# Second attention's row sums taken from the channel sum of its result, with values raised by one and the residual lowered by one

## The chip, the cores and the metric

The kernel runs on one core of a Trainium2 chip. The metric is the device time of one execution in microseconds; the median of three runs stands for a kernel. Profiles come from one further execution.

## The reference, cut to what matters

The input x has 8 batches of 128 channels on 48 x 48 positions, all in fp32. With N = 2304 tokens in a batch, the reference computes:

```python
# layer 0: causal attention with projections of the group-normed input
x0 = concat([gn(x), pe])
q, k, v = lrelu(Wq x0 + bq), lrelu(Wk x0 + bk), lrelu(Wv x0 + bv)
attn = softmax(mask(q.T k / sqrt(128))) * mask
x = x + attn v
# layer 1: attention of the normed tokens with themselves, no weights
t = to_tokens(x)                      # (8, 2304, 128)
h = ln(t)                             # over the 128 channels, no scale, no offset
t = t + softmax(h h.T) h
# FFN: product with W, batch statistics over all tokens, a recurrence over tokens
wx = batch_norm(ln(t) W.T)
y[n] = sigmoid(wx[n] + y[n - 1] V.T)
x = from_tokens(t + y)
```

For the change, two facts of the second attention count. Its score matrix h h.T is symmetric. And the 128 channels of each row of h, being layer-normed without an offset, add up to zero.

## The kernel before, in words

A batch's 2304 tokens are cut into NQ = 6 chunks of QC = 384 tokens, and each chunk into QB = 3 blocks of 128. Both attentions take one chunk of queries after the other. For each block of keys a score matmul gives s (128 keys by 384 queries) in PSUM, ScalarE takes the exponential into p, and a product matmul adds p times the values into o, which holds channels by queries in PSUM. No maximum is taken. The denominators are row sums of p, applied to o after it has been turned so that tokens lie on the partitions.

**Order of the work.** `fast_path` (L605) writes the order of all instructions by hand. The main loop (L1418 to L1446) goes through one list of items, (chunk, block) pairs of all batches; in each step it issues the score of item n (`begin`), the product of item n - 3 (`product`, LAG = 3) and at a chunk's end `after`. Everything else is put in as chains of steps: `Stream` (L548) is a planner with modelled costs of VectorE, ScalarE and GpSimd, and `tick` issues up to two steps whose modelled due time has come after each item. Costs that the code gives a step thus decide where later steps stand. The list of batch b + 1 begins before that of batch b has ended: its first three causal items lie among the last six items of batch b.

**Projections.** `project` (L855) makes q, k and v of a chunk: `normed` (L872), three matmuls pj (L879 and L882), for each an addition z (L884) on VectorE that frees the PSUM bank, and the leaky ReLU (L889). Scores s and projections pj share a pool of four PSUM banks (`ps_s`); turned results share one of two (`ps_t`), and o has two. Tiles p come from a pool of six.

**First attention.** `Causal` (L989): score L1018, exponential L1020, on the diagonal blocks a mask on GpSimd (L1023), product L1029. Its denominators are added up on VectorE in acc (L1040, L1044), and at a chunk's end summed (`turn` L1069 and L1071; `sums` L1077 to L1082, with a matmul against `same`, a matrix that adds up groups of partitions, and a mask `mine` that keeps a partition's own group). `residual` (L1091) gives t1, token by channel, held in t1_tok; moments, a root on GpSimd (L929) and `normed` (L934) give h, stored token major as x_hat[b][0] (xhT in the profile, the values of the second attention), and `back` transposes it into x_hat[b][1] (xh, its queries and keys).

**Second attention.** `Full` (L1123). Since the scores are symmetric, the exponentials of a pair of chunks i < j are made once, as direct tiles (score L1219, exponential L1221 with the running row sums `accum_out` into rows, product L1233). Each such tile is also turned by VectorE in 32 x 32 squares (L1182) into t, stored to DRAM as e (L1162), loaded as g (L1153) and used for the other chunk of the pair (product L1229, "turned"). For every three turned tiles one VectorE reduce (L1190) adds up the sums of the turned part into tsum.

At a chunk's end `after` (L1239) copies o to SBUF (L1251) and adds a chain of steps. `sums` reduces rows (L1259); for chunks 0 to 4 it multiplies tsum by `same` (ts, L1264), keeps its own groups (own, L1269), reduces and adds them (more, L1273, L1274); the reciprocal (L1276) is ri. `residual` turns the result by three transposes on TensorE (of_t, L939), forms t2 = of_t x ri + t1 (L1286, three instructions), takes the moments (L920, L921, L923) and turns t2 (tt, L1293). Then come a root on GpSimd (L1299), DRAM transfers that bring t2 back channel major, `product` (matmul wx L1325, its scaling L1326, statistics L1327) and `stored` (a ScalarE copy L1331). The last two chunks of the last batch take a way without DRAM (L1361 to L1372), and then the recurrence (from L1448) begins.

Tiles of the chain are shared: `chunk_tile(tag, name, holder, steps)` makes the planner run the tile's former chain up to `steps` steps before the tile is taken again, and `st.advance(before, 7)` in `keep` does the same for the chain of the chunk before; these counts include the step `sums`.

Of the kernel before, what the change touches and what calls it, by code (L numbers as in the profile page):

```python
# [14 lines left out]
F32 = mybir.dt.float32  # L15
AF = mybir.ActivationFunctionType
# [588 lines left out]
def fast_path(ctx: ExitStack, tc: tile.TileContext, x, pe, w_ffn, out, x_tok, w_qkv, w_pos, v_t, gamma_beta, flag):  # L605
# [61 lines left out]
    with ExitStack() as actx:  # L667
# [93 lines left out]
        for r in range(1 - R, R):  # L761
            nc.gpsimd.affine_select(
                out=same, in_=same, compare_op=ALU.not_equal, fill=1.0, base=r * SQ, pattern=[[0, R], [-1, SQ]], channel_multiplier=1
            )
        mine = apool.tile([P, NQ - 1, R, QB], F32, tag="mine", name="mine")
        nc.gpsimd.memset(mine, 1.0)
        nc.gpsimd.affine_select(
            out=mine, in_=mine, compare_op=ALU.is_ge, fill=0.0, base=0, pattern=[[0, NQ - 1], [-SQ, R], [0, QB]], channel_multiplier=1
        )
        nc.gpsimd.affine_select(  # L770
            out=mine, in_=mine, compare_op=ALU.is_ge, fill=0.0, base=SQ - 1, pattern=[[0, NQ - 1], [SQ, R], [0, QB]], channel_multiplier=-1
        )
# [216 lines left out]
        class Causal:  # L989
# [57 lines left out]
            def after(self, j, o):  # L1047
# [25 lines left out]
                def sums():  # L1073

                    tp = psum_t(f"dn_{b}_{j}")
                    k = R * QB
                    nc.tensor.matmul(tp[:, :k], same.rearrange("p a c -> p (a c)"), c["parts"], start=True, stop=True)  # L1077
                    own = small.tile([P, R, QB], F32, tag="ownc", name=f"ownc_{b}_{j}")
                    nc.vector.tensor_mul(own.rearrange("p a g -> p (a g)"), tp[:, :k], mine[:, 0].rearrange("p a g -> p (a g)"))
                    ri = small.tile([P, QB], F32, tag="ric", name=f"ric_{b}_{j}")  # L1080
                    nc.vector.tensor_reduce(ri, own.rearrange("p a g -> p g a"), AX.X, ALU.add)
                    nc.vector.reciprocal(ri, ri)  # L1082
                    c["ri"] = ri
# [24 lines left out]
                def back():  # L1108
                    tp = transposed(c["y"], f"tb_{b}_{j}")
                    nc.scalar.copy(x_hat[b][1][:, cols], tp[:, :QC])  # L1110

                c["chain"] = normed_chunks[b, j] = st.add([
                    *through[:1],
# [5 lines left out]
                    (normed, 0.0, [("DVE", 1.1)]),  # L1119
                    (back, 0.35, [("ACT", 0.5)]),  # L1120
                ], max(at, st.free["DVE"]) + 0.2 - st.now)

        class Full:  # L1123
# [6 lines left out]
            def __init__(self, b):  # L1130
                self.b = b
                self.tsum, self.tiles, self.stored, self.loaded = {}, {}, {}, {}
                self.pairs = [(i, j) for j in range(NQ) for i in range(j)]
                self.used, self.to_store = 0, deque()
# [38 lines left out]
            def turned(self, j, m, p, ready):  # L1173

                b = self.b
                n, g = divmod(m, QB)
                if g == 0:
                    if len(self.to_store) > 1:
                        self.store()
                    self.tiles[n] = tpool.tile([P, R, QB, QB, SQ], F32, tag="t", name=f"t_{b}_{j}_{n}")  # L1180
                t = self.tiles[n]
                nc.vector.transpose(  # L1182
                    t[:, :, :, g, :].rearrange("p b j r -> p j b r"), p.rearrange("p (j b r) -> p j b r", j=QB, b=R)
                )
                at = st.then(ready, [("DVE", 0.57)])
                if g == QB - 1:
                    self.to_store.append((j, n, t, at))
                    if j not in self.tsum:
                        self.tsum[j] = small2.tile([P, NQ - 1, R * QB], F32, tag="tsum", name=f"tsum_{b}_{j}")
                    nc.vector.tensor_reduce(  # L1190
                        self.tsum[j][:, n - j - 1, :], t.rearrange("p b j m r -> p (b j) (m r)"), AX.X, ALU.add
                    )
                    st.then(at, [("DVE", 1.35)])
                    del self.tiles[n]

            def begin(self, j, what, first):
                b = self.b
                if first and j == 0:
                    self.rows = small2.tile([P, NB, NQ], F32, tag="rows", name=f"rows_{b}")
                if j == 0:  # L1200
# [19 lines left out]
                p = pp.tile([P, QC], F32, tag="p", name=f"p1_{b}_{j}_{m}")  # L1220
                nc.scalar.activation(p, s[:, :QC], AF.Exp, bias=shift, accum_out=self.rows[:, m, j : j + 1])  # L1221
                return p, st.then(st.spend(QC * US), [("ACT", 0.58)])

            def product(self, j, what, o, p, ready, first, last):
# [7 lines left out]
                else:  # L1232
                    nc.tensor.matmul(o[:, :QC], xhT[:, what[1], :], p, start=first, stop=last)  # L1233
                    st.then(ready, [("ACT", 0.2)])
                    if what[1] // QB > j:
# [3 lines left out]
            def after(self, j, o):  # L1239
                b, rows, tsum = self.b, self.rows, self.tsum  # L1240
                cols = ts(j, QC)
# [3 lines left out]
                if far:  # L1245
                    ot = turn_result(o, f"f_{b}_{j}", c, True)
                    at = st.then(st.now, [("DVE", 0.57)])
                    through = token_major(c, ot, f"f_{b}_{j}", "tof", 4)
                else:
                    o_sb = chunk_tile("o", f"of_{b}_{j}", c, 2)  # L1250
                    nc.scalar.copy(o_sb, o[:, :QC])  # L1251
                    at = st.then(st.now, [("ACT", 0.5)])
                    through = []
                F = len(through)

                def sums():

                    dn = small2.tile([P, QB], F32, tag="dn", name=f"dn_{b}_{j}")
                    nc.vector.tensor_reduce(dn, rows[:, QB * j : QB * (j + 1), : j + 1], AX.X, ALU.add)  # L1259
                    n = NQ - 1 - j  # L1260
                    if n:
                        tp = psum_t(f"ts_{b}_{j}")
                        k = n * R * QB
                        nc.tensor.matmul(  # L1264
                            tp[:, :k], same.rearrange("p a c -> p (a c)"), tsum[j][:, :n, :].rearrange("p n k -> p (n k)"),
                            start=True, stop=True,
                        )
                        own = small2.tile([P, NQ - 1, R, QB], F32, tag="own", name=f"own_{b}_{j}")
                        nc.vector.tensor_mul(  # L1269
                            own[:, :n].rearrange("p n a g -> p (n a g)"), tp[:, :k], mine[:, :n].rearrange("p n a g -> p (n a g)")  # L1270
                        )
                        more = small2.tile([P, QB], F32, tag="more", name=f"more_{b}_{j}")
                        nc.vector.tensor_reduce(more, own[:, :n].rearrange("p n a g -> p g (n a)"), AX.X, ALU.add)  # L1273
                        nc.vector.tensor_add(dn, dn, more)  # L1274
                    ri = small.tile([P, QB], F32, tag="ri", name=f"ri_{b}_{j}")
                    nc.vector.reciprocal(ri, dn)  # L1276
                    c["ri"] = ri

                def residual():
                    tp = None if far else transposed(o_sb, f"of_t_{b}_{j}")  # L1280
                    t2 = chunk_tile("t2", f"t2_{b}_{j}", c, 5 if last else 2 + F, bufs=1)
                    for g in range(QB):
# [8 lines left out]
                    if not last:  # L1291
                        c["tt"] = chunk_tile("turn", f"tt_{b}_{j}", c, 5 + F, bufs=1)
                        nc.vector.transpose(  # L1293
# [21 lines left out]
                def fetch():  # L1315
                    c["t2x"] = chunk_tile("t2x", f"t2x_{b}_{j}", c, 7 + F, bufs=1)
                    nc.sync.dma_start(c["t2x"], t2_d[:, b, cols])
                    c["scale"] = chunk_tile("scale", f"scale_{b}_{j}", c, 8 + F, bufs=1)
                    nc.sync.dma_start(c["scale"], c["rs_d"][0].partition_broadcast(P))
# [13 lines left out]
                def normed():  # L1333
                    c["x2"] = chunk_tile("t2x", f"x2_{b}_{j}", c, 6, bufs=1)
                    normalize(c["x2"], c["t2"], c["mv"], c["rs"])
# [3 lines left out]
                def keep(t2x):  # L1339

                    k = j % (SG // SJ)
                    if before is not None:
                        st.advance(before, 7 if k else len(before.steps) + before.done)
                    if k == 0:
# [13 lines left out]
                def back():  # L1358
                    tp = turned_back(c["x2"], f"tx_{b}_{j}")
                    c["xc"] = chunk_tile("scale", f"xc_{b}_{j}", c, 7, bufs=1)  # L1360
                    nc.scalar.copy(c["xc"], tp[:, :QC])  # L1361
# [20 lines left out]
                else:  # L1382
# [8 lines left out]
                    *through,  # L1391
                    (sums, 0.15, [("DVE", 0.8)]),
                    (residual, 0.0 if far else 0.35, [("DVE", 3.2)]),
                    (rooted, 0.0, [("POOL", 0.9)]),
# [242 lines left out]
```

## Time and profile before

| | before |
|---|---|
| median of three runs | 1771.99 us (1771.10 to 1772.96) |
| the profiled execution | 1769.93 us |
| its span, from first to last instruction | 1768.1 us |
| granted TensorE clock, mean | 0.993 |
| TensorE busy | 1739.9 us, 98% of the span |
| VectorE busy | 1299.7 us, 74% |
| ScalarE busy | 762.5 us, 43% |
| GpSimd busy | 194.9 us, 11% |

The page of the profile calls the engines PE (TensorE), PEld (its weight loads, which overlap it), DVE (VectorE), ACT (ScalarE), POOL (GpSimd) and SP (SyncE, which issues DMAs). A row of a group names line, engine, operation, output and inputs by the program's names, partitions x elements and how often; behind the bar stand the busy time, the mean of one in ns, and the engine's idle time just before these instructions with what ended it. A row of the timeline begins with the start in us from the span's start and the length of a run of like instructions. An fp32 matmul shows as two records. Between two starts of a matmul of 384 columns lie some 0.645 us where PE is not interrupted. From one batch to the next the same instruction comes 207.66 us later.

### The profile page before, as it was taken

How to read it: one execution, taken by the hardware profiler on the slowest of the kernel's cores; microseconds unless marked ns; L12 is line 12 of the kernel's file. 1: busy time of each engine (PE TensorE's matmuls, PEld its weight loads, DVE VectorE, ACT ScalarE, POOL GpSimd, SP SyncE). 2: the span in 40 equal slices, each digit the busy share in tenths (PEclk: the TensorE clock that was granted, in tenths of full speed). 3: DMA queues.
4: the chain of work that ended last, by engine and by line, in shares of the span. 5: the costliest groups of instructions: out<-in, count | busy, mean ns of one | idle time of the engine just before them, and what ended most of it. 6: DMA issues, size and time to landing. Idle time of an engine off the chain costs nothing.

```text
span 1768.1 us, 22177 instructions
## 1 busy us (share of the span) xinstructions
PE 1739.9 (98%) x6215; PEld 1092.2 (62%) x6215; DVE 1299.7 (74%) x3355; ACT 762.5 (43%) x1836; POOL 194.9 (11%) x301
## 2 busy tenths in 40 slices
PE   9999999999999999999999999999999999999996
PEld 5666566665666566665666656665666656666565
DVE  4868668876887668786687767876687866877467
ACT  2344434443345434444344443454344543444445
POOL 1110011100110001100111001200011001110006
PEclk8999999999999999999999999999999999999998
DMA  3405672257533584156731575334832468116768
GB/s 141 139 23 182 184 203 93 89 184 193 146 103 121 157 235 130 47 167 183 209 99 68 190 197 157 107 108 157 228 120 77 148 183 217 56 46 199 194 231 217
DMA packets 206056, 262.00 MB, mean 148 GB/s; under 512 B 90113, under 2 KB 175010, under 8 KB 205412
## 3 DMA queue, kind: packets, MB, share of 16 engines
q1 hardware_dynamic: 204972, 257.47, 48.2%
q0 software_dynamic: 720, 2.62, 1.0%
q8 instruction: 52, 0.85, 0.2%
q14 instruction: 80, 0.66, 0.1%
q10 hardware_dynamic: 232, 0.40, 0.1%
HBM read 150.24 MB, written 110.17 MB: 147 GB/s over the span
## 4 chain that ended last, share of the span: by engine, by line
PE 96%; DMA 1%; DVE 1%; ACT 1%; issue 0%; SPq 0%; POOL 0%; ACTq 0%; DVEq 0%; POOLq 0%
PE o L1233 19%; PE s L1219 19%; PE s L1018 17%; PE o L1029 17%; PE o L1229 13%; PE pj L879 4%; PE pj L882 2%; PE z L1550 2%; PE wx L1325 2%; PE of_t L939 1%; PE tb L939 1%; PE pb L837 0%; DMA x<-in_x_dram 0%; PE dn L1077 0%; PE ts L1264 0%
## 5 line engine op out<-in xcount | busy, mean ns | idle before, releaser
L1221 ACT ACTIVATE p<-s,shift 128x384 f32<-128x384 f32 x504 | 292.3, 580 | 479.1 <-PE s L1219 464.5
L1020 ACT ACTIVATE p<-s 128x384 f32<-128x384 f32 (+2 forms) x504 | 231.6, 460 | 426.0 <-PE s L1018 372.1
L1219 PE MATMUL s<-xh 128*128 128x384 f32 x1008 | 410.6, 489 | 0.0
L1233 PE MATMUL o<-p,xhT 128*128 128x384 f32 x1008 | 404.2, 488 | 5.8 <-ACT p L1221 5.8
L1018 PE MATMUL s<-q,k 128*128 128x384 f32 (+2 forms) x1008 | 382.1, 461 | 0.1
L1029 PE MATMUL o<-p,vT 128*128 128x384 f32 (+2 forms) x1008 | 377.6, 457 | 0.0
L1229 PE MATMUL o<-g,xhT 128*128 128x384 f32 x720 | 281.3, 489 | 0.5 <-issue 0.5
L1233 PEld LDWEIGHTS o<-p,xhT 128*128 128x128 f32 x1008 | 189.4, 190 | 133.2 <-ACT p L1221 10.3
L1029 PEld LDWEIGHTS o<-p,vT 128*128 128x128 f32 x1008 | 189.2, 191 | 114.3 <-issue 0.6
L1219 PEld LDWEIGHTS s<-xh 128*128 128x128 f32 x1008 | 186.7, 191 | 114.8
L1018 PEld LDWEIGHTS s<-q,k 128*128 128x128 f32 x1008 | 183.2, 191 | 96.9 <-issue 0.9
L1044 DVE TENSOR_TENSOR acc<-acc,p 128x384 f32<-128x384 f32 (+2 forms) x408 | 208.9, 512 | 33.0 <-POOL p L1023 8.7
L1182 DVE STREAM_TRANSPOSE t<-p 128x384 f32<-128x384 f32 x360 | 187.2, 550 | 37.6 <-ACT p L1221 35.9
L1229 PEld LDWEIGHTS o<-g,xhT 128*128 128x128 f32 x720 | 133.6, 191 | 82.5 <-DMA g<-e 0.7
L1190 DVE TENSOR_REDUCE tsum<-t 128x12 f32<-128x1152 f32 x120 | 162.4, 1353 | 4.2
L884 DVE TENSOR_TENSOR z<-pj,pb 128x384 f32<-128x384 f32 x144 | 78.9, 548 | 109.3 <-PE pj L879 92.7
L1023 POOL TENSOR_TENSOR p<-p,triu 128x128 f32<-128x128 f32 x144 | 72.5, 505 | 607.4 <-ACT p L1020 476.5
L1299 POOL TENSOR_TENSOR roots<-ve_f,mhalf 128x3 f32<-128x3 f32 x48 | 40.8, 849 | 520.6 <-DVE ve_f L923 520.6
L1221 ACT ACTIVATION_READ_ACCUMULATOR p<-s,shift 128x1 f32 x504 | 97.2, 193 | 0.0
L879 PE MATMUL pj<-xn,wT 128*128 128x384 f32 x192 | 79.9, 501 | 1.4 <-DVE xn L872 1.4
L929 POOL TENSOR_TENSOR rs_c<-ve_c,mhalf 128x3 f32<-128x3 f32 x48 | 45.4, 947 | 215.6 <-DVE ve_c L923 215.6
L1326 DVE TENSOR_TENSOR scale<-wx,scale 128x384 f32<-128x384 f32 x46 | 25.4, 552 | 55.6 <-PE wx L1325 50.6
(242 smaller groups left out, 1471.0 us busy)
## 6 DMA issues: line engine op xcount, KB each, us to landing
e<-t SPq DMA_DIRECT2D x120, 576.0 KB
g<-e SPq DMA_DIRECT2D x480, 144.0 KB
pb<-posb_d SPq DMA_DIRECT2D x46, 576.0 KB
t1t<-in_x_tok_dram SPq DMA_DIRECT2D x48, 192.0 KB
t_d<-tt SPq DMA_DIRECT2D x184, 48.0 KB
t2x<-t_d SPq DMA_DIRECT2D x46, 192.0 KB
scale<-rs SPq DMA_DIRECT2D x46, 192.0 KB
x<-in_x_dram SPq DMA_DIRECT2D x14, 576.0 KB
```

What stands on the lines that cost most here:

```text
L879: nc.tensor.matmul(ps[:, :QC], wT[:, j, :], xn, start=True, stop=True)
L884: nc.vector.tensor_add(z, ps[:, :QC], c["pb"][:, j, :])
L1018: nc.tensor.matmul(s[:, off:QC], keys[b][:, ts(m, P)], queries[b, j][:, off:], start=True, stop=True)
L1020: nc.scalar.activation(p[:, off:], s[:, off:QC], AF.Exp, scale=SCALE)
L1029: nc.tensor.matmul(o[:, off:QC], vals[b][:, ts(m, P)], p[:, off:], start=first, stop=last)
L1044: nc.vector.tensor_add(a[:, off:], a[:, off:], p[:, off:])
L1182: nc.vector.transpose(t[:, :, :, g, :].rearrange("p b j r -> p j b r"), p.rearrange("p (j b r) -> p j b r", j=QB, b=R))
L1190: nc.vector.tensor_reduce(self.tsum[j][:, n - j - 1, :], t.rearrange("p b j m r -> p (b j) (m r)"), AX.X, ALU.add)
L1219: nc.tensor.matmul(s[:, :QC], xh[:, ts(m, P)], xh[:, ts(j, QC)], start=True, stop=True)
L1221: nc.scalar.activation(p, s[:, :QC], AF.Exp, bias=shift, accum_out=self.rows[:, m, j : j + 1])
L1229: nc.tensor.matmul(out_ap, xhT[:, QB * i + g, :], p, start=first, stop=last)
L1233: nc.tensor.matmul(o[:, :QC], xhT[:, what[1], :], p, start=first, stop=last)
```

## The change

The values of the second attention are raised by one after the queries and keys have been made of them. A chunk's result then is (sum of p x h + sum of p) for each channel; as h sums to zero over the 128 channels, the channel sum of the result is 128 times the row sum of p. So the denominators are taken from the result: in `residual` one reduce over the channels of of_t (in PSUM), a multiplication by 1/128 and a reciprocal. The divided result is too large by one, and the residual t1 is lowered by one for that.

All other ways to row sums of the second attention go: accum_out and rows, tsum and its reduces, the step `sums` with the matmul ts. A new step `shifted`, the last of the causal chain, makes the two additions on GpSimd. Modelled costs and the step counts are fitted to this: the exponential 0.5 instead of 0.58 and 0.2, `residual` 4.0 instead of 0.8 (`sums`) and 3.2, `shifted` 1.2 on GpSimd. `mine` shrinks to what the first attention uses.

```diff
@@ fast_path
-        mine = apool.tile([P, NQ - 1, R, QB], F32, tag="mine", name="mine")
+        mine = apool.tile([P, R, QB], F32, tag="mine", name="mine")
...
@@ Causal.after
+                def shifted():
+
+                    nc.gpsimd.tensor_scalar_add(c["y"], c["y"], 1.0)
+                    nc.gpsimd.tensor_scalar_add(t1_tok[b, j], t1_tok[b, j], -1.0)
+
...
                     (back, 0.35, [("ACT", 0.5)]),
+                    (shifted, 0.0, [("POOL", 1.2)]),
                 ], max(at, st.free["DVE"]) + 0.2 - st.now)
@@ Full.turned
                 if g == QB - 1:
                     self.to_store.append((j, n, t, at))
-                    if j not in self.tsum:
-                        self.tsum[j] = small2.tile([P, NQ - 1, R * QB], F32, tag="tsum", name=f"tsum_{b}_{j}")
-                    nc.vector.tensor_reduce(
-                        self.tsum[j][:, n - j - 1, :], t.rearrange("p b j m r -> p (b j) (m r)"), AX.X, ALU.add
-                    )
-                    st.then(at, [("DVE", 1.35)])
                     del self.tiles[n]
@@ Full.begin
-                nc.scalar.activation(p, s[:, :QC], AF.Exp, bias=shift, accum_out=self.rows[:, m, j : j + 1])
-                return p, st.then(st.spend(QC * US), [("ACT", 0.58)])
+                nc.scalar.activation(p, s[:, :QC], AF.Exp, bias=shift)
+                return p, st.then(st.spend(QC * US), [("ACT", 0.5)])
@@ Full.product
-                    st.then(ready, [("ACT", 0.2)])
@@ Full.after
-                    o_sb = chunk_tile("o", f"of_{b}_{j}", c, 2)
+                    o_sb = chunk_tile("o", f"of_{b}_{j}", c, 1)
...
-                def sums():
...
                 def residual():
                     tp = None if far else transposed(o_sb, f"of_t_{b}_{j}")
-                    t2 = chunk_tile("t2", f"t2_{b}_{j}", c, 5 if last else 2 + F, bufs=1)
+
+                    dn = small2.tile([P, QB], F32, tag="dn", name=f"dn_{b}_{j}")
+                    by_token = c["o"].rearrange("p (k g c) -> p g k c", g=QB, c=SQ) if far else tp[:, :QC].rearrange("p (g c) -> p g c", g=QB)
+                    nc.vector.tensor_reduce(dn, by_token, AX.XY if far else AX.X, ALU.add)
+                    nc.vector.tensor_scalar_mul(dn, dn, 1.0 / P)
+                    ri = c["ri"] = small.tile([P, QB], F32, tag="ri", name=f"ri_{b}_{j}")
+                    nc.vector.reciprocal(ri, dn)
+                    t2 = chunk_tile("t2", f"t2_{b}_{j}", c, 4 if last else 1 + F, bufs=1)
...
-                        st.advance(before, 7 if k else len(before.steps) + before.done)
+                        st.advance(before, 6 if k else len(before.steps) + before.done)
...
-                    (sums, 0.15, [("DVE", 0.8)]),
-                    (residual, 0.0 if far else 0.35, [("DVE", 3.2)]),
+                    (residual, 0.0 if far else 0.35, [("DVE", 4.0)]),
```

Counted instruction by instruction in the built programs, the change takes 192 from VectorE and adds 96 to GpSimd. It also moves steps. In the changed order of each batch the transposes of_t and the residual of a Full chunk come earlier; of_t of chunk 2 stands behind the wx matmul of chunk 0, with nine matmuls to the next wx (of chunk 1), where before it stood directly ahead of the wx of chunk 0. At a batch's end the residual of the last chunk (of_t_b_5) stands between the first two projection parts of the next batch's chunk 4 (pj_4_0 and pj_4_1), where before it stood later, behind pj_4_2 and wx. Once in each batch an added GpSimd pair stands ahead of a causal mask: that of chunk 0, between the masks of p_4_13 and p_4_14.

More of the change, by code (lines that the diff above doesn't have):

```diff
@@ L764, in fast_path @@
             )
-        mine = apool.tile([P, NQ - 1, R, QB], F32, tag="mine", name="mine")
+        mine = apool.tile([P, R, QB], F32, tag="mine", name="mine")
         nc.gpsimd.memset(mine, 1.0)
         nc.gpsimd.affine_select(
-            out=mine, in_=mine, compare_op=ALU.is_ge, fill=0.0, base=0, pattern=[[0, NQ - 1], [-SQ, R], [0, QB]], channel_multiplier=1
+            out=mine, in_=mine, compare_op=ALU.is_ge, fill=0.0, base=0, pattern=[[-SQ, R], [0, QB]], channel_multiplier=1
         )
         nc.gpsimd.affine_select(
-            out=mine, in_=mine, compare_op=ALU.is_ge, fill=0.0, base=SQ - 1, pattern=[[0, NQ - 1], [SQ, R], [0, QB]], channel_multiplier=-1
+            out=mine, in_=mine, compare_op=ALU.is_ge, fill=0.0, base=SQ - 1, pattern=[[SQ, R], [0, QB]], channel_multiplier=-1
         )
@@ L1078, in sums @@
                     own = small.tile([P, R, QB], F32, tag="ownc", name=f"ownc_{b}_{j}")
-                    nc.vector.tensor_mul(own.rearrange("p a g -> p (a g)"), tp[:, :k], mine[:, 0].rearrange("p a g -> p (a g)"))
+                    nc.vector.tensor_mul(own.rearrange("p a g -> p (a g)"), tp[:, :k], mine.rearrange("p a g -> p (a g)"))
                     ri = small.tile([P, QB], F32, tag="ric", name=f"ric_{b}_{j}")
@@ L1131, in __init__ @@
                 self.b = b
-                self.tsum, self.tiles, self.stored, self.loaded = {}, {}, {}, {}
+                self.tiles, self.stored, self.loaded = {}, {}, {}
                 self.pairs = [(i, j) for j in range(NQ) for i in range(j)]
@@ L1197, in begin @@
                 b = self.b
-                if first and j == 0:
-                    self.rows = small2.tile([P, NB, NQ], F32, tag="rows", name=f"rows_{b}")
                 if j == 0:
@@ L1239, in after @@
             def after(self, j, o):
-                b, rows, tsum = self.b, self.rows, self.tsum
+                b = self.b
                 cols = ts(j, QC)
@@ L1247, in after @@
                     at = st.then(st.now, [("DVE", 0.57)])
-                    through = token_major(c, ot, f"f_{b}_{j}", "tof", 4)
+                    through = token_major(c, ot, f"f_{b}_{j}", "tof", 3)
                 else:
-                    o_sb = chunk_tile("o", f"of_{b}_{j}", c, 2)
+                    o_sb = chunk_tile("o", f"of_{b}_{j}", c, 1)
                     nc.scalar.copy(o_sb, o[:, :QC])
@@ L1254, in after @@
                 F = len(through)
-                def sums():
[L1258 to L1277, printed above, removed]
                 def residual():
                     tp = None if far else transposed(o_sb, f"of_t_{b}_{j}")
-                    t2 = chunk_tile("t2", f"t2_{b}_{j}", c, 5 if last else 2 + F, bufs=1)
+                    dn = small2.tile([P, QB], F32, tag="dn", name=f"dn_{b}_{j}")
[5 more added lines that the diff above has]
+                    t2 = chunk_tile("t2", f"t2_{b}_{j}", c, 4 if last else 1 + F, bufs=1)
                     for g in range(QB):
@@ L1291, in residual @@
                     if not last:
-                        c["tt"] = chunk_tile("turn", f"tt_{b}_{j}", c, 5 + F, bufs=1)
+                        c["tt"] = chunk_tile("turn", f"tt_{b}_{j}", c, 4 + F, bufs=1)
                         nc.vector.transpose(
@@ L1315, in fetch @@
                 def fetch():
-                    c["t2x"] = chunk_tile("t2x", f"t2x_{b}_{j}", c, 7 + F, bufs=1)
+                    c["t2x"] = chunk_tile("t2x", f"t2x_{b}_{j}", c, 6 + F, bufs=1)
                     nc.sync.dma_start(c["t2x"], t2_d[:, b, cols])
-                    c["scale"] = chunk_tile("scale", f"scale_{b}_{j}", c, 8 + F, bufs=1)
+                    c["scale"] = chunk_tile("scale", f"scale_{b}_{j}", c, 7 + F, bufs=1)
                     nc.sync.dma_start(c["scale"], c["rs_d"][0].partition_broadcast(P))
@@ L1333, in normed @@
                 def normed():
-                    c["x2"] = chunk_tile("t2x", f"x2_{b}_{j}", c, 6, bufs=1)
+                    c["x2"] = chunk_tile("t2x", f"x2_{b}_{j}", c, 5, bufs=1)
                     normalize(c["x2"], c["t2"], c["mv"], c["rs"])
@@ L1359, in back @@
                     tp = turned_back(c["x2"], f"tx_{b}_{j}")
-                    c["xc"] = chunk_tile("scale", f"xc_{b}_{j}", c, 7, bufs=1)
+                    c["xc"] = chunk_tile("scale", f"xc_{b}_{j}", c, 6, bufs=1)
                     nc.scalar.copy(c["xc"], tp[:, :QC])
```

## The prediction

> **What bounds the kernel now.** I read the busy times first, then the chain of work that ended last.
>
> ```profile
> PE 1739.9 (98%) x6215; PEld 1092.2 (62%) x6215; DVE 1299.7 (74%) x3355; ACT 762.5 (43%) x1836; POOL 194.9 (11%) x301
> ```
>
> ```profile
> PE 96%; DMA 1%; DVE 1%; ACT 1%; issue 0%; SPq 0%; POOL 0%; ACTq 0%; DVEq 0%; POOLq 0%
> ```
>
> PE is busy for 98% of the span, and 96% of the chain is PE. Work taken from DVE or ACT is therefore worth nothing by itself; a matmul taken away, or a place where PE stands idle, counts in full. The groups that the change touches, and POOL rows to price what it adds (columns: busy us, mean ns of one, idle before):
>
> ```profile
> L1190 DVE TENSOR_REDUCE tsum<-t 128x12 f32<-128x1152 f32 x120 | 162.4, 1353 | 4.2
> ...
> L1023 POOL TENSOR_TENSOR p<-p,triu 128x128 f32<-128x128 f32 x144 | 72.5, 505 | 607.4 <-ACT p L1020 476.5 <-DVE tt L1293 130.2
> ...
> L1221 ACT ACTIVATION_READ_ACCUMULATOR p<-s,shift 128x1 f32 x504 | 97.2, 193 | 0.0
> ...
> L1071 DVE TENSOR_REDUCE parts<-ta 128x12 f32<-128x384 f32 x48 | 26.5, 553 | 1.6
> ```
>
> Then PE's waits: what can still be won beside matmuls.
>
> ```profile
> PE o L1233 <- ACT p L1221: 5.8, 8, 1.4
> ```
>
> The Full attention's product waits 8 times for an exponential. The timeline of one (the same in seven batches):
>
> ```profile
> 613.45 1.14 ACT L1331 COPY wx<-scale 128x384 f32<-128x384 f32 x1 [2.61 <-DVE scale L1326]
> ...
> 613.78 0.81 PE L1229 MATMUL o<-g,xhT 128*128 128x384 f32 x2
> ...
> 614.50 0.57 ACT L1221 ACTIVATE p<-s,shift 128x384 f32<-128x384 f32 x1
> ...
> 615.21 0.91 PE L1233 MATMUL o<-p,xhT 128*128 128x384 f32 x2 [0.62 <-ACT p L1221]
> ```
>
> The DVE multiply of chunk 0's wx stands behind the residual of chunk 2, whose of_t comes directly ahead of that wx; the ACT copy behind it idles 2.61 us and holds the exponential that PE needs.
>
> **What the Trainium skill says.** "SBUF — State Buffer", Who interferes with whom: a DVE instruction with two SBUF inputs and a GpSimd instruction that reads SBUF shut each other out for a whole instruction, PE and ACT never. The added POOL steps can so delay DVE; the trace of before has too little POOL work to show it. "GPSIMD Engine Reference", section 3.1: an operation with one input takes 1.03 to 1.8 cycles an element. The trace's two-input mask (505 ns for 128 elements) is dearer. "TensorE: Matmul & The Clock Gate", Part 2: weight loads are pulled ahead of running matmuls, matmuls stay in order. The trace agrees: 1092 us of loads lie inside PE's 98%.
>
> **The change part by part.**
>
> *1. The matmul of sums goes.* Each of 40 chunks (5 of 6, 8 batches) ran ts, two passes as all fp32 matmuls here:
>
> ```profile
> 361.66 0.81 PE L1233 MATMUL o<-p,xhT 128*128 128x384 f32 x2
> 362.31 0.33 PE L1264 MATMUL ts<-tsum,same 128*128 128x60 f32 x2
> 362.47 0.87 PE L1219 MATMUL s<-xh 128*128 128x384 f32 x2
> 363.18 1.13 PE L1233 MATMUL o<-p,xhT 128*128 128x384 f32 x3
> ```
>
> From product to product is 363.18 − 361.66 = 1.52 us; without ts a pair takes 2 × 0.645 = 1.29. So one costs 0.23 us of PE, and the narrower ones 0.22: 40 × 0.222 = **−8.9 us**, with nothing that hides it.
>
> *2. DVE and ACT.* Gone on DVE: 120 × 1.353 = 162.4 us of tsum, and 40 times own, more and add. Added: 48 × (a reduce of 384 elements, 0.55 by L1071's row, with bounds 0.5 and 0.65 as it reads PSUM, and a 0.17 multiply). Gone on ACT: 504 × 0.193 = 97.2 us. All of it lies beside PE: 0. It matters only where DVE or ACT ends a wait, which is steps 4 to 6.
>
> *3. POOL.* 96 added instructions on 128x384. No row shows one. Bounds: 0.33 us (the skill's 1.03 cycles an element as an estimate) and 1.4 us (interpolated between the two-input rows of 505 ns at 128 and 1840 ns at 512 elements); I take 0.6, the skill's 1.8 cycles. 96 × 0.6 = 58 us: POOL goes from 11% to about 14%, no bound. What stands behind a pair on POOL: the roots, which nothing urgent awaits, and, once in each batch, the mask of a causal score (p_4_14, behind chunk 0's pair). By the order of instructions the mask before ends 3.0 us after that chunk's back-transposes begin; two shifts end at 4.2, the mask at 4.7; its product is due at 6.56. Slack 1.9 us, so PE waits only from about 1.5 us a shift. The shifted y itself is read by a product at least 5 us later. Cost 0. Two locks of DVE of up to 1.2 us together are covered by the six p tiles; without that cover up to 1.2 us a chunk.
>
> *4. The stall above goes.* In the changed order the residual of chunk 2 comes earlier, behind the wx of chunk 0 instead of ahead of it, and nine matmuls lie between it and the next wx; scale is no longer late. One place costs (615.21 − 613.78 − 0.645) + (615.96 − 615.21 − 0.645) = 0.79 + 0.10 = 0.89 us; 7 × 0.89 = **−6.2 us**. Next late there is nothing: ACT has idled 2.61 us before that copy.
>
> *5. The batch's end gets worse.* In the order of before, the residual of the last Full chunk (2.77 us of DVE) runs after wx, late in causal chunk 2 of the next batch:
>
> ```profile
> 891.97 0.85 DVE L1286 SCALAR_TENSOR_TENSOR t<-of_t,ri,t1t 128x128 f32<-128x128 f32 x3
> ...
> 894.74 0.25 DVE L1044 TENSOR_TENSOR acc<-acc,p 128x128 f32<-128x128 f32 x1
> ```
>
> In the changed order it stands on DVE between the first two projection parts of chunk 4 (pj_4_0 and pj_4_1), with reduce, multiply and reciprocal ahead of it, about 3.7 us in one piece. I summed DVE's list by these rows from the first part of chunk 3 on: of_t ends 8.1, reduce 9.1, multiply 9.7, reciprocal 9.9, residual done 12.85, then an accumulation 13.3, ta and parts 13.9, two accumulations 15.1, and the z add of pj_4_1 frees its PSUM bank at 16.1. Masks, exponentials and six p tiles hide part; a score that needs that bank is due at 15.3 (+0.83), and another waits 0.1 for an exponential whose p tile is freed late. About 0.93 us at each of seven ends: **+6.5 us**. Bounds: 0 (my durations are starts to starts, and the four banks give more room than I count) and 1.55 a place, 11 us.
>
> *6. Head and tail.* At the end of the last batch reduce, multiply and reciprocal come after of_t, in series with everything; before, they were done by 1696.25, ahead of it (1697.22). 0.55 + 0.2 + 0.2 = **+0.95 us**. The eighth wait for an exponential (1.4 us, at 1693) may stay or go: ±1.4. At the head `mine` is smaller: 0.
>
> Sum: −8.9 − 6.2 + 6.5 + 0.95 = −7.65. The profiled execution took 1769.93 us (span 1768.1 and 1.8 around it), so 1762.3; it lies 2.06 below the median of 1771.99, so **1764.3**.
>
> **The rivals.** *B, the batch's end hides its residual*: steps 1, 4 and 6 alone, −14.15, 1757.8. For it: PE never waits in the trace at these ends although ACT there already waits up to 2.2 us for DVE. *C, little is left*: at 1.9 us an end, 7 × 1.9 = 13.3 and the sum is −0.85, 1771.1; or the change doesn't move the stall of step 4 as I read it, −1.45, 1770.5. Against: DVE has 25% of its time free, and gets 162 us more. *D, slower*: DVE's backlog at the batch's end. The 3.7 us piece meets chunk 0's pair on POOL: at 1.4 us each and under the lock, 2.8 us more fall on accumulations that free the p tiles, so exponentials, then scores wait: 0.93 + 2.8 = 3.7 us an end, 26 us in all, sum +12, **1784**. It decides from (14.15 + 3.5) / 7 = 2.5 us an end. Against: price and lock must both stand at their upper ends.
>
> **How the numbers follow.** 0.2% is 3.5 us, about what a measurement of this kernel can tell from no change. My forecast 0.50 (its own range 1760.5 to 1768), B 0.22, C 0.15, D 0.13. Faster: 0.50 + 0.22 + 0.03 of C = 0.75; same 0.12; slower 0.13. The range runs from B less the tail's 1.4 and some spread, 1755.5, to C's centre, 1771.5, and leaves out D and half of C.
>
> **What would show it.** Matmul count down by 80 and PE busy by about 9 us; the 0.62 us waits for ACT at L1221 gone in seven batches; new PE waits of under 1 us for DVE z or ACT p shortly after each batch's end; the added POOL row near 600 ns, with DVE rows beside it no longer; 0.95 us more between of_t and the last moments. I am wrong if a POOL shift takes over 1.5 us, if DVE rows lengthen through the batch, or if the batch ends lose over 2 us each.

## The result, and the profile after

| | before | after |
|---|---|---|
| median | 1771.99 us (5 runs, 1771.10 to 1774.39) | 1761.73 us (5 runs, 1757.80 to 1763.73) |
| profiled execution, span | 1769.93, 1768.1 us | 1763.07, 1761.4 us |
| clock of that execution | 0.993 | 0.991 |

The ratio is 0.9937, with a 95% interval of 0.9922 to 0.9953: faster by 0.6%. The forecast was 1764.3. The engines, and the chain, of the changed kernel:

```profile
PE 1733.7 (98%) x6134; PEld 1082.0 (61%) x6135; DVE 1159.5 (66%) x3163; ACT 718.9 (41%) x1332; POOL 321.0 (18%) x397
...
PE 96%; DMA 1%; DVE 1%; SPq 1%; issue 0%; ACT 0%; POOL 0%; DVEq 0%; ACTq 0%; POOLq 0%
```

VectorE lost 140 us of busy time and ScalarE 44 (the records of the accumulator reads add up to the predicted 97, but lie in part beside other instructions). PE is still busy for 98%: it sets the time as before. The groups (columns as before):

```profile
L1114 POOL TENSOR_SCALAR xhT<-xhT 128x384 f32<-128x384 f32 x48 | 60.8, 1267 | 187.5 <-PE tb L939 187.5
...
L1258 DVE TENSOR_REDUCE dn<-of_t 128x3 f32<-128x384 f32 x48 | 26.6, 554 | 67.5 <-PE of_t L939 67.5
L1115 POOL TENSOR_SCALAR t1t<-t1t 128x384 f32<-128x384 f32 x48 | 61.3, 1277 | 0.0
```

The reduce over the channels costs the 0.55 us that was taken for it. An addition on GpSimd costs 1.27 on the mean, twice what I took. PE's waits, those between the head and the recurrence that pass 1 us:

```profile
PE wx L1306 <- DMA t2x<-t_d: 1.3, 1, 1.3
PE tx L947 <- DVE x L934: 1.3, 1, 1.3
PE o L1227 <- DMA g<-e: 1.1, 2, 0.9
PE o L1231 <- ACT p L1219: 1.1, 1, 1.1
```

Of the eight waits for an exponential (5.8 us) one is left, and all four lines lie in the last batch. Inside the batches this view shows no wait any more; this is a stretch of 207 us in the windows view, first of before, then of after (PE busy is the second number):

```profile
253.00:460.00 207.00, 206.37 (x730) 128.26 (x730) 155.40 (x409) 88.69 (x213) 20.11 (x31) 1.00 0.50 147
```

```profile
253.00:460.00 207.00, 207.00 (x729) 128.16 (x728) 139.15 (x387) 84.55 (x153) 35.95 (x43) 1.00 0.52 149
```

**Where the time went, by stage.** I took from both timelines the first score of each batch's second attention, the last such score's way to the end, and the head before the first:

| stretch | before | after | difference |
|---|---|---|---|
| head, to the first score of the first second attention | 120.32 | 123.75 | +3.43 |
| seven batch periods | 7 x 207.66 | 7 x 205.89 | -12.4 |
| from there in the last batch to the end | 194.17 | 196.38 | +2.2 |

The head is not the change, as a second profile shows below (experiment 11): it is the clock that this execution was granted early on. Without it the change is worth 12.4 - 2.2 = 10.2 us; by the second profile, with 205.90 us a batch and 196.90 at the end, it is 9.6.

### The profile page after: what moved, and what is told of

The parts are those of the page before. It is cut to its first block, busy times and chain, and to the rows that moved or that the text cites. A ratio compares the mean times of both kernels' runs of the same rounds, so it can differ in the third digit from the quotient of the medians.

```text
span 1761.4 us, 21442 instructions
## 1 busy us (share of the span) xinstructions
PE 1733.7 (98%) x6134; PEld 1082.0 (61%) x6135; DVE 1159.5 (66%) x3163; ACT 718.9 (41%) x1332; POOL 321.0 (18%) x397
## 4 chain that ended last, share of the span: by engine, by line
PE 96%; DMA 1%; DVE 1%; SPq 1%; issue 0%; ACT 0%; POOL 0%; DVEq 0%; ACTq 0%; POOLq 0%
PE s L1217 18%; PE o L1231 18%; PE s L1018 17%; PE o L1029 17%; PE o L1227 13%; PE pj L879 4%; PE pj L882 2%; PE z L1530 2%; PE wx L1306 2%; PE tb L939 1%; PE of_t L939 1%; PE pb L837 0%; DMA x<-in_x_dram 0%; PE dn L1077 0%; DMA t2x<-t_d 0%; DMA out_dram<-r 0%
## 5 line engine op out<-in xcount | busy, mean ns | idle before, releaser
L1044 DVE TENSOR_TENSOR acc<-acc,p 128x384 f32<-128x384 f32 (+2 forms) x408 | 213.4, 523 | 26.5 <-POOL p L1023 2.9
L1023 POOL TENSOR_TENSOR p<-p,triu 128x128 f32<-128x128 f32 x144 | 77.8, 544 | 528.9 <-ACT p L1020 527.6
L1114 POOL TENSOR_SCALAR xhT<-xhT 128x384 f32<-128x384 f32 x48 | 60.8, 1267 | 187.5 <-PE tb L939 187.5
L1258 DVE TENSOR_REDUCE dn<-of_t 128x3 f32<-128x384 f32 x48 | 26.6, 554 | 67.5 <-PE of_t L939 67.5
L1115 POOL TENSOR_SCALAR t1t<-t1t 128x384 f32<-128x384 f32 x48 | 61.3, 1277 | 0.0
```

The source lines that it names most:

```text
L1023: nc.gpsimd.tensor_mul(p[:, off : off + P], p[:, off : off + P], triu)
L1044: nc.vector.tensor_add(a[:, off:], a[:, off:], p[:, off:])
```

## The experiments

Periods are those between first scores, in one profiled execution of each kernel; they repeat within 0.05 us from batch to batch unless said. Medians are set against runs of the kernel before on the same chip.

**1. The matmul ts alone.** In the kernel before ts is taken out.

```diff
-    nc.tensor.matmul(tp[:, :k], same..., tsum[j][:, :n, :]..., start=True, stop=True)
...
-    nc.vector.tensor_mul(own..., tp[:, :k], mine...)
+    nc.vector.tensor_mul(own..., tsum[j][:, :n, :]..., mine...)
```

> The kernel before without the matmul ts alone; the instruction that read its result reads tsum instead, so the denominators lack a part, and every other instruction keeps its place. Theory (a matmul on a busy TensorE counts in full, the stall at wx goes by the order): the batch period falls by 5 x 0.2215 = 1.11 us from 207.66 to 206.55, the seven 0.62 us waits for the exponential stay, in all -8.9 us. Rival (the gain comes from the work taken off VectorE and ScalarE): the period stays within 0.3 us of 207.66, since that work is all still there.

Measured: period 206.55 (-1.11), waits for the exponential 5.6 us in 8 places, median 1761.11, ratio 0.9955 (0.9941 to 0.9969). Five ts matmuls a batch cost 0.222 us each, as worked out, and the work on the other engines is no part of it.

**2. The lighter VectorE and ScalarE alone.** No reduces into tsum and no accum_out; ts and the small reduces read constants.

```diff
-    nc.vector.tensor_reduce(self.tsum[j][:, n - j - 1, :], t..., AX.X, ALU.add)
...
-    nc.scalar.activation(p, s[:, :QC], AF.Exp, bias=shift, accum_out=self.rows[:, m, j : j + 1])
+    nc.scalar.activation(p, s[:, :QC], AF.Exp, bias=shift)
```

> The kernel before without the tsum reduces (120 x 1.353 us of VectorE) and without the accumulator reads (504 x 0.193 us of ScalarE); ts and the small reduces read constants in their place, so the denominators are constants; the order of all that is left is that of before. Theory: the period stays at 207.66 us within 0.2 or so and the 0.62 us waits stay, since the multiply at wx still stands behind the residual; in all within 1.5 us of before. Rival (less work on VectorE and ScalarE is what helps): the waits for the exponential go and the period falls by 0.9 us or more, 6 us in all.

Measured: period 207.57 (-0.09), waits 5.3 us in 8 places, ratio 1.0001 (0.9994 to 1.0008). 260 us of work taken from two engines are worth nothing in the old order.

**3. The order alone, with the old work.** The kernel before with the changed kernel's modelled costs and counts.

```diff
-    (sums, 0.15, [("DVE", 0.8)]),
-    (residual, 0.0 if far else 0.35, [("DVE", 3.2)]),
+    (sums_residual, 0.0 if far else 0.35, [("DVE", 4.0)]),
...
-    return p, st.then(st.spend(QC * US), [("ACT", 0.58)])
+    return p, st.then(st.spend(QC * US), [("ACT", 0.5)])
```

> All work of the kernel before, with its planner's costs and step counts set to those of the changed kernel, so that TensorE, VectorE and ScalarE take their instructions in the changed order. Nothing is left out. Theory: the 0.62 us waits go (-0.89 us a batch), ts stays (+0), so the period falls to about 206.8; against that the heavier VectorE list at the batch's end may stall scores by 0.2 to 1 us. So 206.8 to 207.6, and in all -6 to 0 us; the last batch loses 2 to 3 us as in the changed kernel if that loss comes from the order. Rival (order does nothing by itself): period 207.66 with the waits in place.

Measured: period 206.53 in five of seven (206.76 and 207.01 in two, where a statistics matmul, gn_v, comes late on PE by 0.24 and 0.48 us in all), waits at wx gone in the first seven batches, ratio 0.9956 (0.9940 to 0.9973). That is -1.13, more than the 0.89 of the stall. The reason stands in this kernel's timeline of PE:

```profile
792.16 0.32 PE L1262 MATMUL ts<-tsum,same 128*128 128x48 f32 x2
792.31 0.51 PE L939 MATMUL of_t<-ident,of 128*128 128x128 f32 x3
792.66 0.81 PE L1228 MATMUL o<-g,xhT 128*128 128x384 f32 x2
```

From ts to the product behind of_t pass 0.50 us; of_t alone takes 0.33 in the changed kernel. Directly ahead of these transposes, where all five ts of a batch now stand, ts thus costs 0.17 us, not 0.22: five times 0.05 beside the 0.89 make the -1.13. Single effects thus don't add up: -1.11 (ts) and -1.13 (order) are together -1.77. Of their sum of -2.24 the 0.24 of the cheaper ts count twice, and another 0.24 are lost to what the change adds (0.20 at the batch's end and 0.04 by the additions, below).

**4. The new work in the old order.** The changed kernel with the modelled costs of before.

```diff
-    (residual, 0.0 if far else 0.35, [("DVE", 4.0)]),
+    (lambda: None, 0.15, [("DVE", 0.8)]),
+    (residual, 0.0 if far else 0.35, [("DVE", 3.2)]),
...
+    st.then(at, [("DVE", 1.35)])
```

> All work of the changed kernel, with the planner's costs and step counts of before, so that the instructions stand in the order of before (the two GpSimd additions go directly behind the back-transposes); nothing is left out. Theory (two parts, the matmul ts and the order, that don't depend on the lighter engines): the 0.62 us waits at wx are back and ts is gone, so the period is 206.4 to 206.6, 0.6 us above the changed kernel; in all 3 to 5 us slower than it if the last batch loses less in this order. Rival (the lighter VectorE and ScalarE lists make the stall go): 205.9 or less.

Measured: period 207.8 to 208.2, median 1774.54, ratio 1.0020 (1.0011 to 1.0029): slower than before. My expectation missed by 1.4 us a batch. The waits for the exponential are not back at 0.62 but at 1.54 us; this kernel's timeline at the wx of chunk 0:

```profile
817.29 0.56 DVE L1256 TENSOR_REDUCE dn<-of_t 128x3 f32<-128x384 f32 x1 [3.65 <-PE of_t L939]
...
821.08 0.52 DVE L1305 TENSOR_TENSOR scale<-wx,scale 128x384 f32<-128x384 f32 x1
...
821.64 1.14 ACT L1310 COPY wx<-scale 128x384 f32<-128x384 f32 x1 [3.66 <-DVE scale L1305]
...
822.68 1.05 ACT L1216 ACTIVATE p<-s,shift 128x384 f32<-128x384 f32 x2
...
823.32 0.91 PE L1228 MATMUL o<-p,xhT 128*128 128x384 f32 x2 [1.54 <-ACT p L1216]
```

The new reduce, multiply and reciprocal (0.9 us) stand in the same piece of VectorE ahead of the multiply at wx, so that ScalarE's copy, and the exponential behind it, come 0.9 us later. That is 0.9 of the 1.4 us; another 0.3 are lost around the batch's end, where a score waits for a late exponential (PE's starts at 901.99 and 902.42), and the rest, up to 0.4, in some batches before products with a loaded g. PE's waits show none for a mask on GpSimd. The work that the change adds to `residual` more than eats the gain of ts; the order that came with it is what makes it pay: 207.9 against 205.89.

**5. The reduce made twice**, to load the batch's end and the tail.

```diff
     nc.vector.tensor_reduce(dn, by_token, AX.XY if far else AX.X, ALU.add)
+    nc.vector.tensor_reduce(dn, by_token, AX.XY if far else AX.X, ALU.add)
```

> The changed kernel with the reduce over the channels made twice (the same result is written again; nothing is left out). Theory: the VectorE piece at a batch's end grows from 3.8 to 4.35 us, so the exponential behind it comes 0.55 us later, and the score that now loses 0.2 us there loses 0.5 to 0.8: the period rises by 0.3 to 0.6 us; at the end of the last batch 0.55 us more stand in series; in all +3 to +5 us. Rival (VectorE has a third of its time free and the batch's end has room left): the period stays at 205.89 within 0.1, in all +0.6 us.

Measured: period 206.49 (+0.60; 206.83 in one of seven), median 1764.42, ratio 0.9975 (0.9964 to 0.9986). PE's waits have a new line, seven times, and the wait in the tail grows from 1.3 to 1.9:

```profile
PE s L1018 <- ACT p L1020: 3.7, 7, 0.5
...
PE tx L947 <- DVE x L934: 1.9, 1, 1.9
```

So the batch's end has no room left: what is added there on VectorE now counts one for one.

**6. The residual of the batch's end put later**, together with experiment 10's edits.

```diff
-    ], max(at, st.free["DVE"]) + 0.2 - st.now)
+    ], max(at, st.free["DVE"]) + 0.2 - st.now + (4.0 if j == NQ - 1 and b < B - 1 else 0.0))
```

> The kernel of e7_tail with one more edit: the chain of the last chunk of each batch but the last is due 4 us later, so that its residual stands behind the second projection part of chunk 4 instead of ahead of it; nothing is left out. Theory (the VectorE piece of 3.8 us at the batch's end costs 0.2 us of PE by a late exponential): behind the z addition, with the causal chunk further on, it either costs nothing, period 205.7, or meets the accumulations there, period up to 206.5; only its place on VectorE decides. Rival (the 0.2 us have another source): 205.89 unchanged.

Measured: period 205.60 in five of seven (-0.29); 206.04 and 207.01 in two, where PE waits for loads of g (1.3 us in three places; two more in the last batch bring it to 3.2). The two late starts at the batch's end are gone from the trace, and so is the wait for the mask (0.04 us). Median 1757.41, ratio 0.9918 (0.9899 to 0.9938), no different from experiment 10. The 0.2 us of the batch's end were the place of that residual; what they are worth to the whole is within the spread.

**7. GpSimd's additions made twice.**

```diff
-    nc.gpsimd.tensor_scalar_add(c["y"], c["y"], 1.0)
-    nc.gpsimd.tensor_scalar_add(t1_tok[b, j], t1_tok[b, j], -1.0)
+    for _ in range(2):
+        nc.gpsimd.tensor_scalar_add(c["y"], c["y"], 0.5)
+        nc.gpsimd.tensor_scalar_add(t1_tok[b, j], t1_tok[b, j], -0.5)
```

> The changed kernel with each GpSimd addition made twice, of half the amount; nothing is left out. Theory (only what stands behind an addition on GpSimd can hold TensorE, and the only such place is the causal mask behind chunk 0's pair, which is now just late): GpSimd busy rises by about 122 us, and in each batch the mask and the product behind it come 2.4 us later, less what slack is left: the period rises from 205.89 by 1.5 to 2.6 us, 12 to 20 us in all. Rival (GpSimd has 80% of its time free, so more work there is hidden): the period stays within 0.2 us of 205.89.

Measured: period 207.9 to 208.5, +2.3 (210.2 in the first), median 1784.34, ratio 1.0074 (1.0059 to 1.0089). GpSimd is at 24%, and yet it holds PE. Its waits, and GpSimd's timeline at one of them:

```profile
PE o L1029 <- POOL p L1023: 18.0, 9, 2.2
```

```profile
928.00 1.17 POOL L1116 TENSOR_SCALAR t1t<-t1t 128x384 f32<-128x384 f32 x1
929.14 0.45 POOL L1023 TENSOR_TENSOR p<-p,triu 128x128 f32<-128x128 f32 x1
```

That is the mask behind chunk 0's additions; PE's product starts at 929.65 with 2.05 us of waiting.

**8. The additions in blocks of 128 columns.**

```diff
-    nc.gpsimd.tensor_scalar_add(c["y"], c["y"], 1.0)
-    nc.gpsimd.tensor_scalar_add(t1_tok[b, j], t1_tok[b, j], -1.0)
+    for src, by in ((c["y"], 1.0), (t1_tok[b, j], -1.0)):
+        for g in range(QB):
+            nc.gpsimd.tensor_scalar_add(src[:, ts(g, P)], src[:, ts(g, P)], by)
```

> The changed kernel with each GpSimd addition on 128x384 cut into three on 128x128; nothing is left out. It tells a fixed cost from one by element: if an addition costs a + 384 b = 1.18 us undisturbed with a = 0.1, three take 1.38; if a is 0.3, three take 1.8. The mask behind chunk 0's pair comes later by 0.4 to 1.3 us, so the period rises by 0.3 to 1.2 us if the theory of the late mask holds, and stays at 205.89 if GpSimd's work is hidden.

Measured, in a single execution of 1767.80 us: period 206.5 to 206.6 in five of seven (206.97 and 207.53 in two, with waits for loads of g), +0.6 to +0.7. As in experiment 7, the product behind chunk 0's mask waits (3.9 us in 8 places). One block has a median of 0.53 us, against 1.17 to 1.18 for 384 columns. So 2.5 ns for each further column and 0.21 us fixed, and three blocks take 1.6.

**9. No additions.** The sums are then not the row sums of p; a constant is added to them that keeps the reciprocal finite.

```diff
-    nc.gpsimd.tensor_scalar_add(c["y"], c["y"], 1.0)
-    nc.gpsimd.tensor_scalar_add(t1_tok[b, j], t1_tok[b, j], -1.0)
+    pass
...
-    nc.vector.tensor_scalar_mul(dn, dn, 1.0 / P)
+    nc.vector.tensor_scalar(dn, dn, 1.0 / P, 1e27, ALU.mult, ALU.add)
```

> The changed kernel without the two GpSimd additions of every chunk (the values are not raised, the denominators are then not the row sums; a constant is added to keep them finite). The order of all else stays. Theory: the additions cost TensorE 0.05 to 0.25 us a batch by the mask and the accumulations behind them, so the period falls from 205.89 to 205.65 to 205.84, 0.4 to 2 us in all. Rival (GpSimd and VectorE shut each other out and the additions cost several us): the period falls by 0.5 us or more, 4 us in all.

Measured: period 205.85 (-0.04), ratio 0.9947 (0.9931 to 0.9964). The additions cost PE 0.04 us a batch, at the lower edge of what I expected. VectorE's accumulations take 519 ns here and 523 with the additions: what the additions take from VectorE is next to nothing in this kernel. The last batch took 198.9 us in this profile, 2.5 longer than with the additions: an exponential came 2.20 us late there, and a low clock followed (last section), so that the medians don't show the 0.04 us.

**10. The last batch.** A tile of its own for the copy of chunk 4, which is due 2.5 us later.

```diff
+    if b == B - 1 and j == NQ - 2:
+        spare = pbp.tile([P, 3, QC], F32, tag="pb", name=f"t2c_{b}_{j}")
...
-    (rooted, 0.0, [("POOL", 0.9)]),
+    (rooted, 0.0, [("POOL", 0.9), ("", 2.5 if last and j == NQ - 2 else 0.0)]),
```

> The changed kernel with two edits for the last batch alone: the copy of t2 of chunk 4 goes to a tile of its own, so that it needn't wait for the store of the tile before, and that step is due 2.5 us later, so that the wx matmul of chunk 3 stands behind its loads. Nothing is left out. Theory (the changed kernel loses 3.3 us in its last batch, of which 1.0 in the series of reduce, multiply and reciprocal and the rest in waits for loads and for an exponential behind that copy): the waits of 1.3 us for t2x and 1.1 us for the exponential go, -2 to -2.7 us in all, about 1759.3. Rival (those waits only move to the next step of the same chain): within 0.5 us of the changed kernel, 1761.7.

Measured: the last batch takes 193.3 us from its first score to the end, against 196.4 and 196.9; both waits are gone; median 1757.58, ratio 0.9931 (0.9918 to 0.9945). Its last batch is thus 3.1 to 3.6 us faster than that of the changed kernel. The medians show less: it lies 12.3 us below the kernel before on its own chip, the changed kernel 10.3 (first runs) and 10.1 (experiment 11), and the intervals of the ratios overlap. So it is the stage that shows the gain, not the whole time.

**11. The changed kernel again.**

> The changed kernel once more, for a second profile and more runs of it. Theory (the 3.4 us that the first profile of it lost before the first second attention are the clock that TensorE was granted early in that execution, not the change): the batch period is 205.89 us again, the time to the first score of the second attention differs from 123.75 us by what the granted clock between 30 and 45 us differs, and at the same mean clock the runs lie 10 to 11 us below those of before. Rival (the change makes the head slower): 123.7 us again.

Measured: periods 205.86 to 205.91; head 120.88 us; median 1760.36, ratio 0.9940 (0.9924 to 0.9957). The same kernel has two heads, and the clock explains them (windows of 30 to 45 us, first profile and second; the clock stands behind POOL's count):

```profile
30.00:45.00 15.00, 14.76 (x39) 7.88 (x40) 6.13 (x15) 3.40 (x7) 0.16 (x1) 0.68 0.23 78
```

```profile
30.00:45.00 15.00, 14.71 (x51) 8.60 (x52) 7.35 (x18) 3.89 (x8) 0.45 (x1) 0.89 0.34 117
```

0.21 x 15 = 3.2 us, and the heads differ by 2.87. The rival, a slower head by the change, is out: experiments 5 and 10, whose head is that of the changed kernel, took 119.0 and 120.4 us for it, at clocks of 0.92 and 0.89, and experiment 2, with the old order, took 123.6 at 0.67. In runs of equal mean clock the spread shrinks: at 0.992 eleven runs of before have a mean of 1772.7 us and six of the changed kernel 1760.7, a difference of 12.0; at 0.994 it is 1768.7 (15 runs) to 1757.8 (one), 10.9.

## Why the prediction was right or wrong

| step | predicted | measured | from |
|---|---|---|---|
| 1, ts goes | -8.9 | -8.9 | experiment 1, 8 x 1.11 |
| 2, work off VectorE and ScalarE | 0 | 0 | experiment 2 (-0.09 a batch) |
| 3, GpSimd's additions | 0 | +0.3 | experiment 9, 7 x 0.04 |
| 4, the stall at wx | -6.2 | -6.2 | waits gone, 7 x 0.89 |
| 5, the batch's end | +6.5 | +1.4 | 7 x 0.20 in the trace |
| 6, last batch | +0.95 | +3.3 | +2.2 and the 1.1 of its five ts |
| sum | -7.65 | -10.1 | stages without the head: -10.2 |

The time fell into the range and near the forecast, but in part because errors cancelled, and that is luck: step 5 was 5 us too dear, step 6 took 2.4 too little. That the profiled execution, 1763.07, lies still nearer to the 1762.3 forecast for it is luck too, by 3.4 us of low clock in its head. At the batch's end, the step that set the forecast apart from rival B, rival B was nearer: of 6.5 us 1.4 came.

**Step 5 failed on one assumption**: that "the z add of pj_4_1 frees its PSUM bank at 16.1" and a score "that needs that bank is due at 15.3 (+0.83)". VectorE's list came out about as summed (the z addition ends 0.6 us earlier against the reduce), PE's wait didn't come. VectorE's timeline after:

```profile
669.24 0.55 DVE L1258 TENSOR_REDUCE dn<-of_t 128x3 f32<-128x384 f32 x1
...
673.03 0.52 DVE L1040 TENSOR_TENSOR acc<-p,p 128x384 f32<-128x384 f32 x1
...
675.66 0.55 DVE L884 TENSOR_TENSOR z<-pj,pb 128x384 f32<-128x384 f32 x1
```

and PE's:

```profile
674.18 0.91 PE L1018 MATMUL s<-q,k 128*128 128x384 f32 x2
...
675.58 0.59 PE L1018 MATMUL s<-q,k 128*128 128x256 f32 x2
...
678.81 0.83 PE L882 MATMUL pj<-wT,xn 128*128 128x128 f32 x6
```

and ScalarE's:

```profile
673.64 0.87 ACT L1020 ACTIVATE p<-s 128x384 f32<-128x384 f32 x2 [3.60 <-DVE acc L1040]
```

The piece takes 673.03 - 669.24 = 3.79 us (3.7 predicted). The z addition runs from 675.66 to 676.2, and the score that I had put into its bank starts at 675.58, before it, without a wait: it uses another bank. In the built program the six scores behind pj_4_1 take turns in the other three banks, and the bank that this z frees goes to the next projection part, pj_4_2, at 678.81, 2.6 us later. I had taken the four banks to go round in the order of allocation and not looked up what that score waits for. What remains is the second part of the step, the exponential whose p tile is freed late: it waits 3.60 us for the accumulation behind the residual, and the score at 674.18 waits for the bank that it reads; there and at the next start PE loses 0.10 us each (0.1 predicted in all). Experiment 5 shows that this part is real and now at its edge.

**Step 3 was right in effect, wrong in size.** 0.6 us an addition measured 1.27. The Trainium skill, "GPSIMD Engine Reference", section 3.1, names some 1.8 cycles an element as the best case of a tight loop, which I had read as the upper end for one input: as an estimate from it 384 columns take 0.58 us, where they took 1.17, and experiment 8 gives 2.5 ns for each further column and 0.21 us fixed. The measurement decides. The point from which PE waits, "about 1.5 us a shift", held roughly: with 1.18 and 1.53 us for the pair the mask is just late,

```profile
707.54 1.53 POOL L1115 TENSOR_SCALAR t1t<-t1t 128x384 f32<-128x384 f32 x1
709.05 0.62 POOL L1023 TENSOR_TENSOR p<-p,triu 128x128 f32<-128x128 f32 x1
```

and doubled (experiment 7) nearly all of it reaches PE. Taking the 0.33 to 1.4 us as a range was worth more than the value chosen. The lock that the Trainium skill describes in "SBUF — State Buffer", Who interferes with whom, fits what the trace shows: of the 96 additions the 31 longest (1.42 to 1.55 us) all run beside an accumulation of VectorE, which has two inputs in SBUF, and the 47 beside none take 1.16 to 1.18; 18 run beside one and are not longer. Accumulations of 384 columns take 588 ns beside an addition and 555 elsewhere. So the lock, if it is that, costs an addition up to 0.4 us and not a whole instruction, and PE nothing beyond the 0.04 us of experiment 9; rival D, which built on it, is refuted in its size.

**Step 4 held, for a reason that needs the order.** That the stall goes is shown by experiment 3; that it goes by the order and not by lighter engines, by experiments 2 and 4. What I hadn't said is that in the old order the same work would have doubled it.

**Step 6 was right in its term and missed its company.** The serial part shows as the wait of tx, 1.3 us for 0.3 before: +1.0 (0.95 predicted). Most of the other 2.3 us are waits for loads (t2x 1.3, g 1.1, none of them before) less what the wait for the exponential shrank (1.4 to 1.1). In the last batch the chain of chunk 4 pulls that of chunk 3 along through `keep`; t2x of chunk 3 is issued at 1674.18 us, behind 12 loads of g on SP's queue:

```profile
1668.01 6.07 SPq L1159 DMA_DIRECT2D g<-e  x12
1674.18 0.38 SPq L1298 DMA_DIRECT2D t2x<-t_d  x1
```

Before, t2x stood behind as many loads, and wx 4.4 us behind its issue (1683.66 to 1688.04); ScalarE's copy, which waits for the same load, could start at 1687.9, 4.2 us after the issue, so PE found it there. Now wx would stand 4.1 us behind the issue, and the copy starts at 1679.73, 5.5 us after it. So 0.3 us are the chain's, which is due earlier behind its own DMA, and 1.3 the load's, which took that much longer. In the second profile of the same kernel (experiment 11) the copy starts 4.9 us after the issue and wx waits 0.8: a part of the 1.3 belongs to this one execution, and why the load takes longer is open. I had moved the residual and not followed its chain to the DMA that it forces. Experiment 10 takes these waits away.

## What to carry to other kernels

When one engine is busy for 98%, price a change by what it takes off that engine and by the waits it moves, and count nothing for the rest, however many microseconds it is. When a change to modelled costs moves steps, price the work in the new order: here the same work loses 3 to 4 us in one order and gains 10 in the other. Before a stall is charged to a shared buffer, look up which instruction really waits for it; and follow a moved step to the last DMA that its chain forces.

## What the runs showed of the hardware

- A GpSimd addition of a constant to fp32, 128 partitions: 0.53 us for 128 columns and 1.17 for 384; beside an accumulation of VectorE with two inputs in SBUF up to 1.55, and never over 1.18 where none runs beside it (96 additions of the changed kernel).
- A short matmul costs by what stands behind it: ts 0.22 us ahead of a matmul of 384 columns, 0.17 ahead of transposes of 128 (experiments 1 and 3).
- The clock granted between 30 and 45 us of a run was 0.67 to 0.92, whatever the kernel, and two profiles of the changed kernel differ by 3 us for it, where its runs spread over 5.9.
- In experiment 9, after PE had been idle for 2.20 us in the last batch, the clock was 0.62 over the next 4.5 us (matmuls of 384 columns took 0.64 us a pass instead of 0.32, for 3.2 us). In experiment 7 PE idles nine times for 1.7 to 2.2 us: after two such places the clock was low (0.94 over 28 us around the one at 91.41 us, 0.91 over 20 around the one at 303.55, which makes most of the 2 us by which that kernel's first period is longer), and after the seven others it was 1.00. The Trainium skill, "TensorE: Matmul & The Clock Gate", Part 1, tells of a monitor that halves the clock by how busy PE was in a free-running window of about 3.4 us. The half speed agrees, and so does its length: 0.38 x 4.5 us are 1.7 us of lost clock, which is 3.4 us at half speed. That idle times of one length are hit twice and spared seven times fits a window that runs free.
